# Turning more GRU state by DMA in a four-layer graph network, with a new planned order

## The chip, the cores and the metric

The kernel runs on one core of a Trainium2 chip. A core has a matrix engine (TensorE, PE in the profile; PEld is its loading of weights), a vector engine (VectorE, DVE), a scalar engine (ScalarE, ACT), GpSimd (POOL) and SyncE (SP), which here only issues DMAs. Each engine works through its own list of instructions in order and waits on semaphores for the others. The metric is device time in microseconds of one execution; the time of a kernel is the median of its runs.

## The reference

The input is 64 graphs of 256 nodes with 256 features in float32, and for each graph a 256 x 256 adjacency matrix of zeros and ones. Four layers follow each other, each of the form `x = x + f(relu(layernorm(x)), adj)`:

- layer 0: graph attention with 4 heads of 64. Scores are leaky-ReLU of a source score plus a destination score, masked by the adjacency, softmax over neighbours, then ELU.
- layer 1: graph attention with 4 heads, ReLU and a second layer norm over each head.
- layer 2: graph attention with one head of 256.
- layer 3: a gated graph network with three rounds, which share the GRU weights:

```
for i in range(3):
    m = h @ weight[i]
    aggr = A.T @ m
    h = gru_cell(aggr, h)     # r, z = sigmoid(...), n = tanh(i_n + r * h_n), h = (1 - z) * n + z * h
```

All is float32 in the reference.

## The kernel before

The 64 graphs are taken in 33 units: the first and the last hold one graph, the 31 between hold two (`units`, line 853). For a unit the function `graphs` (line 1053) records the operations of `layer0`, `layer1`, `layer2` and `gru`. Nothing runs while it records: `op` (line 600) notes an engine, a cost in ns, the buffers read and written, and a function that will emit the instructions. Most operations are emitted through a helper, so the profile shows them at line 906.

The planner `_Schedule` then sets the order. `plan` (line 696) walks backwards from the end that each unit is given, `(first + nb) * PACE / 2` (line 1664), and gives each operation a due time. `run` (line 706) simulates the engines with the recorded costs: whenever an engine is free it starts the operation with the earliest due time whose inputs are done and whose buffers are free. The order found is the order in which the instructions are written out, for every engine and for the queues on which SP and ACT issue DMAs. Constants shape it: `HOP` is the time from the end of an operation until others may use it, `RESERVE` multiplies costs, `DMA_LATENCY` (3500 ns) and `DMA_RATE` price a DMA, `YIELD` says when DVE leaves the SBUF port that it shares with GpSimd. Buffers come from classes with fixed counts (line 888): for example 5 `xt` (the rows of a unit), 8 PSUM banks, 2 `hl`, one `am_r`, 2 `y`, 3 `pl`, 2 `tp`. Classes in `STRICT` (only `hl`) are not given to a later unit while an earlier one still has to take one.

Attention. Rows are normalised (`norm`), turned so that features lie on partitions (`transposed`), and multiplied by the weights (`project`, line 1200). Attention weights are products of exponentials, so each needs one multiplication and a maximum (`weights`, line 1291). A head can be "lifted": ACT computes the first part (line 1306) and DVE one fused operation per 256 columns. Otherwise DVE does a multiplication with maximum (line 1297) and a minimum with the mask. `LIFTED0` names the lifted heads for units 0 to 2, `LIFTED` for the others.

The GRU. State and aggregate are held with features on partitions, in two halves j = 0, 1 of 128 features. `gate` (line 1551) multiplies gate weights with the state `ht` (weights `whh`) or the aggregate `ag` (weights `wc`): two products, each seen in the trace as two MATMUL records. In a round, `unit` (line 1615) computes each half of the new state `h_new`. For the next round its rows are needed with nodes on partitions: `rows_of` (line 1581) turns a half and `split` (line 1511) writes it as a high part and a remainder (`hl`), rounded to a format that PE multiplies faster; `aggregate` (line 1525) multiplies by the adjacency (`am_r`) and copies the result to `ag`.

A half is turned in one of two ways. On PE: four transposes into a PSUM bank (line 1590). By DMA, in `rows_turned` (line 1560): ACT copies the float32 half into two planes of 16-bit numbers (`pl`, line 1149), SP issues a DMA that transposes 2-byte elements (`tp`, line 1570), and DVE joins the planes into `y`. For units 1 to 31 (`BACK`) the DMA way is used for both halves after the last round and for the halves named in `EARLY` after rounds one and two. The first and last unit use PE. After the last round the turned half is added to `xt`, and the unit's `xt` is stored by one DMA (line 1653). `transposed` uses the same three steps for units 3 to 31.

At the start the gate biases `bih` and `bhh` are loaded on ACT's queue (lines 961 and 962) and added on DVE by `gate_biases` (line 1044).

Of the kernel before, what the change touches and what calls it, by code (L numbers as in the profile page):

```python
# [14 lines left out]
OP = mybir.AluOpType  # L15
# [507 lines left out]
CLOSED = 0  # L523
CENTRED = ()
BACK = range(1, 32)
EARLY = (0,)
HEADS = 3
LIFTED0 = (0,)
CENTRED0 = ()
SPLIT_DVE = ()  # L530
JOIN_DVE = ("y",)
HI_DVE = False
MERGED = True
LIFTED = (0,2)
LEAVE = 0
PACE = 97000.0


def _runs(numbers):
# [15 lines left out]
class _Op:  # L555
    __slots__ = (
        "engine", "cost", "port", "emit", "group", "bufs", "takes", "nbytes", "succs", "waits", "due", "ready",
        "index", "yields", "base", "grabs", "leave", "halves",
    )


class _Schedule:
# [9 lines left out]


    OVERLAP = {"pe": 0, "act": 97, "dve": 81, "pool": 0, "sp": 0}
    HOP = {"pe": 300, "act": 100, "dve": 60, "pool": 100, "sp": 0}
    DMA_LATENCY = 3500
    DMA_RATE = 220.0
    DMA_AHEAD = 2000
    RESERVE = {"dve": 1.0, "act": 1.03}
    STRETCH = 1.0  # L580
    MARGIN = 1600
    YIELD = 5000.0
    GUARDED = ("wh","cb2_")
    STRICT = ("hl",)
    STICK = 0.0
# [12 lines left out]
        return _Buf(cls, shape, dtype, tile)  # L598

    def op(self, engine, cost, emit, reads=(), writes=(), takes=(), nbytes=0, port=False, yields=False,  # L600
           grabs=False, leave=0, halves=False):
        o = _Op()
        o.leave, o.halves = leave, halves
        o.port, o.yields, o.grabs = port or grabs, yields, grabs
        o.engine, o.base, o.emit, o.group, o.nbytes = engine, cost, emit, self.group, nbytes
        o.cost = cost * self.RESERVE.get(engine, 1.0)
        o.succs, o.index, o.ready = [], len(self.ops), 0.0
        deps, o.bufs, o.takes = set(), [], []
        for written, items in ((False, reads), (True, writes)):
            for item in items:  # L610
                b, part = item if isinstance(item, tuple) else (item, None)
                if b not in o.bufs:
                    o.bufs.append(b)
                    b.left += 1
                if written and b.tile is None and b not in o.takes:
                    o.takes.append(b)
                keys = list(b.parts) if part is None else [k for k in (part, None) if k in b.parts]
                for k in keys:
                    writer, readers = b.parts[k]
                    if writer is not None:  # L620
                        deps.add(writer)
                    if written:
                        deps.update(readers)
                writer, readers = b.parts.get(part, (None, []))
                if written:
                    if part is None:
                        b.parts.clear()
# [68 lines left out]
    def plan(self):  # L696
        for o in reversed(self.ops):
# [2 lines left out]
                if s.group == o.group or o.group not in self.end or o.group < 0:  # L700
                    late = min(late, s.due - self.STRETCH * s.cost - self.MARGIN)
            if o.nbytes:
                late -= self.DMA_LATENCY + o.nbytes / self.DMA_RATE
            o.due = late

    def run(self):
# [28 lines left out]
        while True:  # L735
# [74 lines left out]
def _fast_path(  # L810
# [86 lines left out]
    buf, op = sched.buf, sched.op  # L897
# [17 lines left out]
    def dma(engine, nbytes, emit, reads=(), writes=(), takes=(), cost=None):  # L915
        op(engine, cost or (450 if engine == "sp" else 320), emit, reads, writes, takes, nbytes)

    a_t = [buf("ag", [P, 2, H, E]) for _ in range(2)]
    a2_t = buf("o", [P, 4, H, E])
# [133 lines left out]
    def graphs(u, first, nb):  # L1053
# [165 lines left out]
        def factors(wh, heads, width, slope, shift):  # L1219
# [29 lines left out]
                for h in range(heads):  # L1249
                    spread(h)  # L1250
            else:
                ps, row, rd = bank(), buf("row", [R, P]), buf("rd", [R, P])

                def emit_t():
                    nc.tensor.transpose(  # L1255
                        ps.tile[:R, :P], wh.tile.rearrange("p h c w -> p (h c) w")[:, :, width + 1], ident
                    )

                op("pe", 109, emit_t, [wh], [ps])

                def emit_row():
                    nc.scalar.activation(
                        row.tile, ps.tile[:R, :P], AF.Exp, scale=slope - 1.0, bias=-shift * (slope - 1.0)
                    )

                op("act", 260, emit_row, [ps], [row])
                dma("act", 1 << 13, lambda: nc.scalar.dma_start(rd.tile, row.tile), [row], [rd])

                def broadcast(k, cb):
                    dma("sp", K * nb << 17, lambda: nc.sync.dma_start(  # L1270
# [234 lines left out]
        def gru(pair):  # L1505

            xt, hns, am_h = pair["xt"], pair["hn"], pair["am"]
            am = buf("am_r", [P, C, N], F32R)
            vec(nc.vector.tensor_copy, dve(683), lambda: am.tile, lambda: am_h.tile, reads=[am_h], writes=[am], port=True)

# [70 lines left out]
            def rows_of(ht, j, last):  # L1581
# [27 lines left out]
            for i in range(L):  # L1609
# [51 lines left out]

    for u, (first, nb) in enumerate(units):
        sched.group = u
        sched.end[u] = (first + nb) * PACE / 2
        graphs(u, first, nb)


# [70 lines left out]
```

## Time and profile before

| | us |
|---|---|
| median of 3 runs | 3004.19 (3002.52 to 3005.85) |
| the profiled execution's own time | 3004.92 |
| its span, first to last instruction | 3003.1 |
| mean granted TensorE clock | 0.998 |
| gates, line 1553: busy | 2124.5 in 4752 MATMUL records |
| transposes of state, line 1590: busy | 41.8 in 272 |
| ACT copies into pl from the state | 128.9 in 124 (1040 ns each) |
| DVE copies into y | 91.1 in 124 (735 ns each) |
| DMA transposes tp<-pl of all layers | 356 issues |

A line of the profile's groups gives source line, engine, operation, output and inputs by the program's names, and shapes. Matmuls are pipelined and their ends are modelled, so the busy time of a short group includes a drain that overlaps the next one; in the chain of work each group is counted only until the next begins. SPq marks an instruction that SP's queue issues. A wait is put down to the semaphore that came last.

### The profile page before, as it was taken

To read this page: it belongs to the slowest core of one execution; us is meant where nothing else is said; L and a number is where in the kernel's file an instruction comes from. 1 tells how busy PE (TensorE), PEld (TensorE's weight loads), DVE (VectorE), ACT (ScalarE), POOL (GpSimd) and SP (SyncE) were. 2 spreads that over 40 slices of the span, in tenths; PEclk is the share of its full clock that TensorE was granted. 3 is DMA by queue.
4 is the path that set the end of the run, shared out by engine and by line. 5 is a ranking of instruction groups with operands and counts; after the bars stand their busy time and mean duration, and the time that the engine had idled before them with its cause. 6 is when DMAs were issued, how large, how long until landed. Compare 5 with 4: busy or idle time off the path is not lost.

```text
span 3003.1 us, 47684 instructions
## 1 busy us (share of the span) xinstructions
PE 2969.4 (99%) x17175; PEld 1783.2 (59%) x17175; DVE 2330.5 (78%) x5547; ACT 2313.0 (77%) x4321; POOL 279.5 (9%) x317
## 2 busy tenths in 40 slices
PE   8999999999999999999999999999999999999998
PEld 6765556555556556566555565556565565565555
DVE  7878877778877788877778777788777788777754
ACT  7867788778788787878878788787887877776653
POOL 2101001011010101000100100110101010000000
PEclk9999999999999999999999999999999999999999
DMA  4323333434343333334333244343333333322210
GB/s 131 79 57 73 76 85 78 92 67 97 71 92 71 85 86 76 89 79 81 92 69 91 67 85 92 74 93 72 91 68 85 88 79 78 77 57 68 46 38 19
DMA packets 494793, 232.12 MB, mean 77 GB/s; under 512 B 421642, under 2 KB 474452, under 8 KB 494548
## 3 DMA queue, kind: packets, MB, share of 16 engines
q1 hardware_dynamic: 490576, 227.62, 33.2%
q8 instruction: 138, 2.26, 0.3%
q10 hardware_dynamic: 3972, 1.36, 0.2%
q14 instruction: 107, 0.88, 0.1%
HBM read 109.84 MB, written 17.34 MB: 42 GB/s over the span
## 4 chain that ended last, share of the span: by engine, by line
PE 98%; DVE 1%; ACT 0%; DMA 0%; issue 0%; SPq 0%; ACTq 0%; DVEq 0%
PE bank L1553 66%; PE bank L1332 12%; PE bank L1200 12%; PE bank L1532 6%; PE bank L1590 1%; PE bank L1026 1%; PE bank L1235 0%; PE bank L1161 0%; PE bank L1255 0%; DMA w0e<-in_L_gnn_W_dram 0%; DVE o L906 0%; DVE g L906 0%; ACT g L906 0%; DVE xt L906 0%; DVE ht L906 0%
## 5 line engine op out<-in xcount | busy, mean ns | idle before, releaser
L1553 PE MATMUL bank<-ht,whh 128*128 128x512 f32 (+1 forms) x2376 | 1064.5, 580 | 0.8 <-ACT ht L906 0.8
L1553 PE MATMUL bank<-ag,wc 128*128 128x512 f32 (+1 forms) x2376 | 1060.0, 581 | 0.0
L1553 PEld LDWEIGHTS bank<-ag,wc 128*128 128x128 f32 x2376 | 446.4, 190 | 499.2 <-issue 479.5
L1553 PEld LDWEIGHTS bank<-ht,whh 128*128 128x128 f32 x2376 | 436.7, 190 | 442.2 <-issue 424.6
L906 ACT ACTIVATE g<-bank,bg 128x512 f32<-128x512 f32 (+1 forms) x594 | 396.5, 672 | 241.7 <-PE bank L1553 236.3
L906 DVE SCALAR_TENSOR_TENSOR g<-g,g 128x512 f32<-128x512 f32 (+1 forms) x396 | 264.8, 669 | 353.5 <-ACT g L906 351.2
L1332 PEld LDWEIGHTS bank<-wh,pt 128*64 128x64 f32 (+1 forms) x8704 | 342.6, 141 | 82.6 <-issue 64.7
L1332 PE MATMUL bank<-wh,pt 128*64 128x65 f32 (+1 forms) x8704 | 373.1, 232 | 1.7 <-DVE pt L906 1.7
L1306 ACT ACTIVATE pt<-cb,f 128x256 f32<-128x256 f32 x620 | 328.8, 588 | 1.9 <-DMA cb<-rd 1.8
L906 DVE SCALAR_TENSOR_TENSOR pt<-pt,f,cap 128x256 f32<-128x256 f32 x620 | 272.3, 478 | 68.0 <-ACT pt L1306 67.8
L1149 ACT COPY ht<-tp 128x1024 uint16<-128x1024 uint16 x232 | 304.6, 1339 | 1.3 <-DMA tp<-pl 1.3
L1210 ACT ACTIVATE wh<-bank,mv 128x264 f32<-128x264 f32 (+1 forms) x384 | 176.5, 479 | 122.7 <-PE bank L1200 121.9
L1532 PE MATMUL bank<-am_r,hl 128*128 128x256 f32 x1536 | 251.5, 312 | 0.0
L906 POOL TENSOR_TENSOR mv<-mv,nhalf 128x4 f32<-128x4 f32 (+1 forms) x132 | 146.6, 1111 | 1093.1 <-DVE mv L1091 733.2
L1149 ACT COPY pl<-xn 128x1024 uint16<-128x1024 uint16 x232 | 234.9, 1039 | 0.0
L1532 PEld LDWEIGHTS bank<-am_r,hl 128*128 128x128 f32 x1536 | 201.5, 189 | 52.9 <-issue 41.7
L906 ACT ACTIVATE g<-g,bg 128x512 f32<-128x512 f32 (+1 forms) x198 | 139.7, 707 | 95.1 <-DVE g L906 90.8
L906 DVE BATCH_NORM_STATS2 st<-xt 128x6 f32<-128x256 f32 x512 | 183.1, 411 | 7.0 <-DMA xt<-in_x_dram 6.0
L1297 DVE TENSOR_SCALAR pt<-cb,f 128x256 f32<-128x256 f32 x532 | 184.3, 407 | 4.1 <-ACT cb L1243 3.6
L906 POOL TENSOR_TENSOR mean<-mean,nhalf 128x8 f32<-128x8 f32 (+1 forms) x66 | 114.6, 1743 | 739.4 <-DVE mean L906 714.3
L1105 ACT ACTIVATE xn<-xt,mv 128x256 f32<-128x256 f32 x384 | 167.5, 496 | 4.9 <-DVE mv L906 4.1
L906 ACT COPY ag<-bank 128x512 f32<-128x512 f32 (+1 forms) x198 | 109.0, 566 | 79.9 <-PE bank L1532 79.6
(100 smaller groups left out, 3217.8 us busy)
## 6 DMA issues: line engine op xcount, KB each, us to landing
cb<-rd SPq DMA_DIRECT2D x120, 512.0 KB
xt<-in_x_dram SPq DMA_DIRECT2D x31, 512.0 KB
at<-in_adj_dram SPq DMA_DIRECT2D x31, 512.0 KB
out_dram<-xt SPq DMA_DIRECT2D x31, 512.0 KB
cb<-rd SPq DMA_DIRECT2D x34, 256.0 KB
tp<-pl SPq DMA_TRANSPOSE x356
cap<-cap_n SPq DMA_TRANSPOSE x128
rd<-row ACTq DMA_DIRECT2D x60, 8.0 KB
```

The lines of the kernel that those rows point to most:

```text
L906: emit = lambda: fn(*[a() if callable(a) else a for a in args], **kw)
L1026: nc.tensor.matmul(ps.tile[:, :D], lhsT=w3[i].tile[:, ec, dc * P : (dc + 1) * P], rhs=wih[k].tile[:, ec, :], start=(ec == 0), stop=(ec == ...
L1105: op("act", 505, lambda: nc.scalar.activation(view(), xt.tile[:, c, :], AF.Relu, bias=mv.tile[:, 3, c : c + 1], scale=2.0 if MERGED else 1 ...
L1149: op("act", cost, lambda: nc.scalar.copy(to(), of()), reads, writes)
L1200: nc.tensor.matmul(ps.tile[:, : heads * W], lhsT=ht.tile[:, c, dc, :], rhs=we[:, dc].rearrange("p h w -> p (h w)"), start=(dc == 0), stop= ...
L1210: op("act", 470, lambda: nc.scalar.activation(wh.tile[:, :, c, :], ps.tile[:, : heads * W].rearrange("p (h w) -> p h w", h=heads), AF.Iden ...
L1297: nc.vector.tensor_scalar(pt.tile[:, b, jc, :].rearrange("p (i n) -> p i n", n=P), cb.tile[:, k, 2 * b : 2 * b + 2, :], f.tile[:, 1, h, c ...
L1306: op("act", 590, lambda: nc.scalar.activation(view().rearrange("p (i n) -> p i n", n=P), cb.tile[:, k, 2 * b : 2 * b + 2, :], AF.Relu, sca ...
L1332: nc.tensor.matmul(ps[q * Q : (q + 1) * Q], lhsT=pt.tile[:, b, jc, i0 : i0 + Q], rhs=wh.tile[:, h, 2 * b + jc, :w], start=(jc == 0), stop= ...
L1532: nc.tensor.matmul(ps.tile[:, b * N : (b + 1) * N], lhsT=rows(k, b, sc), rhs=am.tile[:, 2 * b + sc, :], start=(k == 0 and sc == 0), stop=( ...
L1553: nc.tensor.matmul(by_chunk(ps.tile[:, :S]), lhsT=w[:, dc, g * P : (g + 1) * P], rhs=block(v, dc), start=(first and dc == 0), stop=(last a ...
L1590: nc.tensor.transpose(ps.tile[:, c * P : (c + 1) * P], ht.tile[:, j, c * P : (c + 1) * P], ident)
```

## The change

- `EARLY` becomes (0,1): after rounds one and two the second half too is turned by DMA in units 1 to 31.
- `LIFTED0` becomes (0,2): head 2 of layers 0 and 1 is lifted for units 0 to 2.
- A DMA can carry a `lag`, a further time by which the planner takes it to land later. The two bias loads get 6000 ns.
- The last unit stores each half of its features when that half is done, instead of one store at the end.
- Buffers: xt 5 to 6, xn 4 to 3, y 2 to 1, pl 3 to 2, tp 2 to 3; a class `col` is declared.
- Planner: PACE 97000 to 100000, HOP of PE 300 to 250 and of DVE 60 to 100, RESERVE of ACT 1.03 to 1.0, YIELD 5000 to 0, a DVE plane copy costed at 738 for 690.
- A second way to form `rd` (`by_columns`) is written but `SCATTER` is False, and `FIRST` is 0, so neither has an effect.

```
-EARLY = (0,)
+EARLY = (0,1)
 HEADS = 3
-LIFTED0 = (0,)
+LIFTED0 = (0,2)
...
+SCATTER = False
 LIFTED = (0,2)
 LEAVE = 0
-PACE = 97000.0
+PACE = 100000.0
+FIRST = 0.0
+LAG = 6000
...
-    HOP = {"pe": 300, "act": 100, "dve": 60, "pool": 100, "sp": 0}
+    HOP = {"pe": 250, "act": 100, "dve": 100, "pool": 100, "sp": 0}
...
-    RESERVE = {"dve": 1.0, "act": 1.03}
+    RESERVE = {"dve": 1.0, "act": 1.0}
...
-    YIELD = 5000.0
+    YIELD = 0.0
...
             if o.nbytes:
-                late -= self.DMA_LATENCY + o.nbytes / self.DMA_RATE
+                late -= self.DMA_LATENCY + o.lag + o.nbytes / self.DMA_RATE
...
-                        post(self.dma_free + self.DMA_LATENCY, "done", o)
+                        post(self.dma_free + self.DMA_LATENCY + o.lag, "done", o)
...
-            "xt": (slots, 5), "at": (slots, 1), "am": (slots, 6), "cap": (slots, 4),
-            "cap_n": (slots, 1), "xn": (slots, 4), "ht": (slots, 2), "wh": (slots, 3),
+            "xt": (slots, 6), "at": (slots, 1), "am": (slots, 6), "cap": (slots, 4),
+            "cap_n": (slots, 1), "xn": (slots, 3), "ht": (slots, 2), "wh": (slots, 3),
...
-            "hl": (slots, 2), "am_r": (slots, 1), "g": (slots, 8), "y": (slots, 2), "f": (slots, 6),
-            "st": (slots, 4), "mv": (slots, 6), "row": (slots, 3), "rs": (slots, 10),
-            "mean": (slots, 4), "pl": (slots, 3), "tp": (slots, 2), "rd": (dram, 4), "bank": (banks, 8),
+            "hl": (slots, 2), "am_r": (slots, 1), "g": (slots, 8), "y": (slots, 1), "f": (slots, 6),
+            "st": (slots, 4), "mv": (slots, 6), "row": (slots, 3), "col": (slots, 4), "rs": (slots, 10),
+            "mean": (slots, 4), "pl": (slots, 2), "tp": (slots, 3), "rd": (dram, 4), "bank": (banks, 8),
...
-    dma("act", 1 << 12, lambda: nc.scalar.dma_start(bi.tile, bih), (), [bi])
-    dma("act", 1 << 12, lambda: nc.scalar.dma_start(bh.tile, bhh), (), [bh])
+    dma("act", 1 << 12, lambda: nc.scalar.dma_start(bi.tile, bih), (), [bi], lag=LAG)
+    dma("act", 1 << 12, lambda: nc.scalar.dma_start(bh.tile, bhh), (), [bh], lag=LAG)
...
-                vec(nc.vector.tensor_copy, 690, to, of, reads=reads, writes=writes, port=True)
+                vec(nc.vector.tensor_copy, 738, to, of, reads=reads, writes=writes, port=True)
...
+            halved = u == len(units) - 1
...
                 vec(nc.vector.scalar_tensor_tensor, dve(685), lambda: xt.tile[:, :, block], view, 0.5,
-                    lambda: xt.tile[:, :, block], op0=OP.mult, op1=OP.add, reads=[ps], writes=[xt])
+                    lambda: xt.tile[:, :, block], op0=OP.mult, op1=OP.add,
+                    reads=[ps, *(parts(xt, range(C)) if halved else [])], writes=[(xt, ("j", j)) if halved else xt])
+                if halved:
+                    dma("sp", nb << 17, lambda: nc.sync.dma_start(
+                        out_v[:, chunks, block], xt.tile[:, :, block]), [(xt, ("j", j))], [])
...
-            dma("sp", nb << 18, lambda: nc.sync.dma_start(out_v[:, chunks, :], xt.tile), [xt], [])
+            if not halved:
+                dma("sp", nb << 18, lambda: nc.sync.dma_start(out_v[:, chunks, :], xt.tile), [xt], [])
```

More of the change, by code (lines that the diff above doesn't have):

```diff
@@ L557 @@
         "engine", "cost", "port", "emit", "group", "bufs", "takes", "nbytes", "succs", "waits", "due", "ready",
-        "index", "yields", "base", "grabs", "leave", "halves",
+        "index", "yields", "base", "grabs", "leave", "halves", "lag",
     )
@@ L600, in op @@
     def op(self, engine, cost, emit, reads=(), writes=(), takes=(), nbytes=0, port=False, yields=False,
-           grabs=False, leave=0, halves=False):
+           grabs=False, leave=0, halves=False, lag=0):
         o = _Op()
-        o.leave, o.halves = leave, halves
+        o.leave, o.halves, o.lag = leave, halves, lag
         o.port, o.yields, o.grabs = port or grabs, yields, grabs
@@ L913, in _fast_path, with dma @@
     B_ids = const(ident)
-    def dma(engine, nbytes, emit, reads=(), writes=(), takes=(), cost=None):
-        op(engine, cost or (450 if engine == "sp" else 320), emit, reads, writes, takes, nbytes)
+    def dma(engine, nbytes, emit, reads=(), writes=(), takes=(), cost=None, lag=0):
+        op(engine, cost or (450 if engine == "sp" else 320), emit, reads, writes, takes, nbytes, lag=lag)
     a_t = [buf("ag", [P, 2, H, E]) for _ in range(2)]
@@ L1251, in factors, with by_rows, emit_t, emit_row @@
             else:
[L1252 to L1267, printed above, removed]
+                rd = buf("rd", [R, P])
+                def by_rows():
+                    ps, row = bank(), buf("row", [R, P])
+                    def emit_t():
+                        nc.tensor.transpose(
+                            ps.tile[:R, :P], wh.tile.rearrange("p h c w -> p (h c) w")[:, :, width + 1], ident
+                        )
+                    op("pe", 109, emit_t, [wh], [ps])
+                    def emit_row():
+                        nc.scalar.activation(
+                            row.tile, ps.tile[:R, :P], AF.Exp, scale=slope - 1.0, bias=-shift * (slope - 1.0)
+                        )
+                    op("act", 260, emit_row, [ps], [row])
+                    dma("act", 1 << 13, lambda: nc.scalar.dma_start(rd.tile, row.tile), [row], [rd])
+                def by_columns():
+                    col = buf("col", [P, heads, C])
+                    op("act", 225, lambda: nc.scalar.activation(
+                        col.tile, wh.tile[:, :, :, width + 1], AF.Exp,
+                        scale=slope - 1.0, bias=-shift * (slope - 1.0),
+                    ), [wh], [col])
+                    dma("act", 1 << 13, lambda: nc.scalar.dma_start(
+                        rd.tile.rearrange("r p -> p r"), col.tile.rearrange("p h c -> p (h c)"),
+                        allow_slow_non_contiguous=True), [col], [rd], lag=9000)
+                by_columns() if SCATTER else by_rows()
                 def broadcast(k, cb):
@@ L1663, in _fast_path @@
         sched.group = u
-        sched.end[u] = (first + nb) * PACE / 2
+        sched.end[u] = (first + nb) * PACE / 2 - (FIRST if u == 0 else 0.0)
         graphs(u, first, nb)
```

## The prediction

> **What bounds the kernel now.** I read the page's busy times and its chain first.
>
> ```profile
> span 3003.1 us, 47684 instructions
> PE 2969.4 (99%) x17175; PEld 1783.2 (59%) x17175; DVE 2330.5 (78%) x5547; ACT 2313.0 (77%) x4321; POOL 279.5 (9%) x317
> ```
>
> PE was busy for 2969.4 of 3003.1 us, and the chain of work that ended last is PE for 98% of the span. Only 33.7 us are not PE's. The next view, busy time by stretch, says where those lie (columns: stretch, its length, then busy us and instruction count of PE, PEld, DVE, ACT and POOL, granted clock, DMA share, GB/s).
>
> ```profile
> 0.00:100.00 100.00, 78.79 (x767) 64.97 (x768) 82.37 (x260) 75.22 (x201) 22.66 (x39) 0.97 0.41 114
> 100.00:2900.00 2800.00, 2799.65 (x16059) 1659.60 (x16059) 2205.54 (x5193) 2196.82 (x4042) 254.78 (x275) 1.00 0.35 78
> 2900.00:3004.00 104.00, 90.93 (x351) 58.67 (x349) 42.63 (x96) 40.98 (x78) 2.03 (x3) 0.98 0.08 19
> ```
>
> The head loses 21.2 us of PE, the tail 12 to 13, and the 2800 us between 0.35. In that middle ACT and DVE have a fifth of their time free, and the granted clock is 1.00. So what leaves PE in the middle leaves the span, as long as the next instruction of PE's fixed list is ready. Whether it is turns on the layer boundary of the GRU; the timeline shows one (start us, us, engine).
>
> ```profile
> 634.12 1.23 SPq L1570 DMA_TRANSPOSE tp<-pl  x1
> 641.14 0.68 DVE L906 SCALAR_TENSOR_TENSOR ht<-g,g 128x512 f32<-128x512 f32 x1
> 641.90 0.71 DVE L906 COPY y<-tp 128x1024 uint16<-128x1024 uint16 x1
> 643.28 0.60 PE L1590 MATMUL bank<-ident,ht 128*128 128x128 f32 x4
> 644.40 0.56 ACT L1519 CAST hl<-bank 128x512 fp32r<-128x512 f32 x1
> 647.74 0.67 DVE L906 TENSOR_TENSOR hl<-bank,hl 128x512 fp32r<-128x512 f32 x1
> 649.45 1.51 PE L1532 MATMUL bank<-am_r,hl 128*128 128x256 f32 x8
> 651.50 0.56 ACT L906 COPY ag<-bank 128x512 f32<-128x512 f32 x1
> 654.26 1.88 PE L1553 MATMUL bank<-ag,wc 128*128 128x512 f32 x4
> ```
>
> The second half of the state is ready at 641.82, is turned on PE at 643.28, and the first gate that needs its aggregate runs at 654.26: 12.4 us, in which PE did other work. The first half went by DMA; its copy into y ran 6.5 us after its issue ended.
>
> **The change, part by part.**
>
> *The PE transposes removed.* Units 1 to 31 turn the second half after layers one and two: 62 groups of four transposes, 248 of the 272 at line 1590. In the chain a group takes 0.44 us, so 62 x 0.44 = 27.3 us. From the other side: by line 1590's busy time, 41.8 us for 272, a group is 0.61, or 38 us; but that counts the drain, which overlaps the next matmul. Without unit 31's two groups, which lie in the tail, it is 26.4. I take -27.3.
>
> *The work added in their place.* Each group now needs a pl copy on ACT (1.04 us), a transpose on SP's queue (1.24 to issue, and by the trace's semaphore records a median of 1.83 more to land), a y copy on DVE (0.735), and the split from y instead of from PSUM (ACT 0.613 for 0.583; DVE 0.680 for 0.676). Over 62 groups ACT gains 64.5 + 1.9 = 66 us, DVE 46, SP's queue 77. In the middle (60 groups) ACT goes from 2197 to 2261 us and DVE from 2206 to 2250, in a stretch shortened to 2774: 82% and 81%. They lie beside PE; I cost them at nothing while PE stays the fullest. If that cover went, the price would be the latency below.
>
> *The latency added at a boundary.* Before: 0.60 + 0.58 + 0.68 = 1.9 us from state to split rows. After: 1.04 + 1.24 + 1.83 + 0.74 + 0.61 + 0.68 = 6.1. That is 4.3 us more, 266 us if all 62 were bare. Cover: in the boundary shown, 641.82 + 6.1 + 0.95 for the aggregate + 0.59 for its copy + about 0.7 for hand-overs gives 650.2, still 4 us before the consumer. At the next boundary the state is ready at 677.92, so the aggregate would be copied by 686.3, where it now is copied by 688.75. Further cover: six hidden-state gates of 1.72 us each depend only on the state; three had run by 654.26. What is late next is the aggregate's copy, not PE. I take 0. Bounds: nothing, to 1 us bare at every boundary (+62).
>
> *What queues behind the new waits.* On ACT the 124 pl copies that wait for the state cost 11.6 us of idling over 29 waits; 62 more make about 6 us, free at 82%. On DVE no y copy waited visibly. On SP a transpose stands in the queue until ACT has filled pl, and loads behind it stand too; yet ACT's lifted weights waited only 1.9 us in all for broadcast loads. I take 0; bounds 0 and +6 from that ACT row.
>
> *Head: second lifted head, later biases.* For units 0 to 2 head 2 of layers 0 and 1 moves from four 0.407 copies and a 1.215 minimum to four 0.588 activations on ACT and four 0.478 on DVE. Counting unit 0 as half size, DVE loses 4.8 us and ACT gains 11.8. From 81.7 to 95.5 us the chain runs mostly over DVE with PE waiting, so relief there can reach PE. Bounds -4.8 (all of it) and +11.8 (all of ACT's). I take -1: the nearest row is that DVE stretch, but only part of the relief precedes it. The bias additions ran at 11.60 directly behind another DVE operation: 0, within 1 us either way.
>
> *The tail.* Unit 31's two groups get the longer path where little else runs. State ready at 2905.64: the aggregate comes at about 2914.0, its consumer now starts at 2912.34, and hidden-state gates are left to fill. Ready at 2932.95: 2941.3 against 2940.61. I take +1; bounds 0 and +6. The last store was issued at 2997.45 and SP saw it land by 3001.50; half of it leaves earlier now, but its data comes from a first half finished 0.7 us before. I take -0.3; bounds -1.5 (the fastest store of the run landed 2.17 us after its issue, this one 3.66) and +0.5 (one more 0.39 us issue).
>
> *Buffers and planner constants.* xt 5 to 6, xn 4 to 3, y 2 to 1, pl 3 to 2, tp 2 to 3, and new costs, hand-over times and pace. No instruction changes; the order does, and no row prices one order against another. Bounds: -12 (over half of the head's idle) to the +62 above; I take 0, since the middle idles 0.35 us in 2800 and a boundary has 4 us of room.
>
> *Sum.* The profiled execution took 3004.9 us (span 3003.1): 3004.9 - 27.3 - 1 + 1 - 0.3 = 2977.3. It stood 0.7 above the median, 3004.19, so about 2977.
>
> *A rule that speaks against it.* The row: a group holds PE 0.44 us, and the DMA takes 1.24 + 1.83 us, held by no compute engine. The Trainium skill's "VectorE: DVE Perf Modes", "The three transpose paths" and "Rules for kernel authors", puts a 128x128 bf16 transpose at 390 ns on TensorE and 1309 ns by DMA, and says to use TensorE when a PSUM destination is acceptable. It is acceptable here. An estimate by that page: eight two-byte blocks by DMA are 10.5 us against 1.6, so 62 x 8.9 = +552 us. The rule compares latencies and doesn't ask which engine is full, so I go by the row.
>
> **The rivals.**
>
> *Slower: the boundary becomes bare.* PE runs its list in order. The GRU uses most of PE (line 1553 alone is 66% of the chain), and with one am_r and the strict hl rule a unit's GRU hardly overlaps the next one's. If the planner finds too little other work within 6 us, or one y or three xn hold it back, each of 62 boundaries stalls. At 1 us that is +62: 2977 + 62 = 3039. It decides from 0.44 us a boundary, where the gain is gone. For it: 4.3 us are added where the room was 4. Against: the trace's 6.5 us from issue to y in the boundary shown did no harm.
>
> *Part of the gain is lost.* ACT is fullest at 75.6 of 91 us (691 to 782) and would reach 78 of 90. If its in-order list makes PE wait 0.25 us at each boundary, 62 x 0.25 = 15: 2992.
>
> *No change.* The relief is taken by another limit, say the wait for the unit's own aggregate, at 0.44 us a boundary: 3004. For it: the removal shortens PE, not the GRU's chain. Against: the room of 4 us.
>
> *More gain.* The new order also closes head idling, up to 12 us: 2965.
>
> **How the numbers follow.** Forecast 2977, its own range 2966 to 2986 (head -10, tail and queues +9): 0.60. More gain, below 2964: 0.02. Part lost, 2986 to 2998: 0.10. No change: 0.07. Slower: 0.21, with about 0.17 beyond 3012. A measurement of this kernel tells about 0.2%, 6 us, from no change. Faster is 0.60 + 0.02 + 0.10 = 0.72. The range runs from 2964 to 3012, leaving out 0.02 and 0.17.
>
> **What would show it.** Line 1590 with 24 transposes, 186 y copies, PE busy near 2942 us; the middle still without PE waits, ACT and DVE near 82%. PE waits at lines 1532 or 1553 on hl or ag, repeating every 30 to 45 us, would show the slower rival. The prediction is wrong if the middle idles over half a microsecond at a boundary.

## The result and the profile after

The changed kernel took 2992.4 us (median of 6 runs, 2989.96 to 2994.56), the kernel before beside it 3004.73 (3002.52 to 3006.56). The ratio is 0.9959, 95% interval 0.9947 to 0.9972: 12.3 us faster. I had forecast 2977, so 27 us faster. The direction and the range (2964 to 3012) held, the size did not: less than half of the gain arrived.

The profiled execution of the changed kernel took 2989.96 us, the fastest of its six and 2.4 under their median; that of the kernel before took 3004.92. Between these two the difference is 15.0 us. From the page, the busy times and the line of the copies that feed the new transposes:

```profile
span 2988.0 us, 47508 instructions
PE 2952.2 (99%) x16927; PEld 1751.9 (59%) x16927; DVE 2380.5 (80%) x5603; ACT 2367.7 (79%) x4403; POOL 274.9 (9%) x317
...
L1152 ACT COPY pl<-ht 128x1024 uint16<-128x1024 uint16 x186 | 193.5, 1042 | 6.1 <-DVE ht L909 5.9
```

The instructions are as announced: 186 copies for 124 on ACT, and 248 PE instructions fewer (17175 to 16927). Of the line that turned state on PE, now line 1608, 24 instructions are left (shortest, median and longest in ns, then the first and last start in us):

```profile
L1608 PE MATMUL bank<-ident,ht x24: 272/273/327, 113.1 to 2981.4; 128*128 128x128 f32 x24
```

ACT and DVE took the work without becoming full (79% and 80%). But PE's busy time fell by 17.2 us, from 2969.4 to 2952.2, where I had said "near 2942". The busy time by stretch (columns: stretch, length, then busy us and count of PE, PEld, DVE, ACT and POOL, granted clock, DMA share, GB/s) shows that this isn't a matter of waiting:

```profile
0.00:100.00 100.00, 79.36 (x781) 66.47 (x782) 81.12 (x260) 81.43 (x213) 23.73 (x39) 0.98 0.42 112
100.00:2900.00 2800.00, 2796.14 (x15846) 1634.01 (x15845) 2261.33 (x5264) 2249.86 (x4120) 250.32 (x276) 1.00 0.37 84
2900.00:2988.00 88.00, 76.68 (x305) 51.45 (x303) 38.05 (x81) 36.46 (x70) 0.80 (x2) 0.97 0.10 24
```

PE idles 20.6 us in the head (21.2 before), 3.9 in the middle (0.35), 11.3 in the tail (12.2 of the 103.1 us to the span's end). That is 2 us more idling in all. The clock is the same. So PE was busy, with fewer instructions, for some 10 us longer than my sum has it. What was it busy with?

**Where the time is.** The timeline of PE shows it (start us, us, line, instruction, count). The attention of layers 0 and 1 multiplies with 64 columns of weights, half of the array's width: `128*64`, 64 records for an operation on two heads. In the kernel before, two such operations often stand back to back:

```profile
726.69 1.88 PE L1553 MATMUL bank<-ag,wc 128*128 128x512 f32 x4
728.50 3.96 PE L1332 MATMUL bank<-wh,pt 128*64 128x65 f32 x128
732.39 2.01 PE L1200 MATMUL bank<-w2e,ht 128*128 128x258 f32 x8
```

In the changed kernel they mostly stand alone, with gates between:

```profile
726.32 3.60 PE L1571 MATMUL bank<-ht,whh 128*128 128x512 f32 x8
729.84 2.09 PE L1349 MATMUL bank<-wh,pt 128*64 128x65 f32 x64
731.86 1.98 PE L1571 MATMUL bank<-ht,whh 128*128 128x512 f32 x4
733.78 2.08 PE L1349 MATMUL bank<-wh,pt 128*64 128x65 f32 x64
735.79 3.70 PE L1571 MATMUL bank<-ht,whh 128*128 128x512 f32 x8
```

Read the starts. A gate record starts every 0.429 us in a long row of them, so four take 1.72 us; the four between the two half-width stretches take 731.86 to 733.78, 1.92. The last record before a stretch and the first behind it each hold PE some 0.1 us longer. And 128 half-width records in one stretch take 3.89 us, two stretches of 64 take 2 x 2.02 = 4.04 (the second: 733.78 to 735.79, 2.01). Over the trace, from the start of the last gate record ahead of a stretch to the start of the second behind it, the median is 3.072 us with 64 half-width records (17 times) and 4.942 with 128 (23 times). So 64 records cost 4.942 - 3.072 = 1.870, and entering and leaving costs 3.072 - 1.870 - 2 x 0.429 = 0.344 us a stretch. Stretches of 32 records check that this doesn't hang on the length: the sum gives 0.935 + 0.858 + 0.344 = 2.137, and the two such in the changed kernel with gates around them take 2.140 and 2.141.

Counted in the trace as unbroken rows of `128*64` records, there are 77 stretches before and 113 after. 36 x 0.344 = 12.4 us. With the 27.3 us of transposes that makes -14.9 us of PE work, and the two profiled executions differ by 15.0. That was an account of two traces; the runs below test it.

### The profile page after: what moved, and what is told of

Read it like the earlier page. It is cut to its first block, busy times and chain, and to the rows that moved or that the text cites. A ratio compares the mean times of both kernels' runs of the same rounds, so it can differ in the third digit from the quotient of the medians.

```text
span 2988.0 us, 47508 instructions
## 1 busy us (share of the span) xinstructions
PE 2952.2 (99%) x16927; PEld 1751.9 (59%) x16927; DVE 2380.5 (80%) x5603; ACT 2367.7 (79%) x4403; POOL 274.9 (9%) x317
## 4 chain that ended last, share of the span: by engine, by line
PE 97%; ACT 2%; DVE 1%; issue 0%; DMA 0%; POOL 0%; DVEq 0%; ACTq 0%; POOLq 0%
PE bank L1571 66%; PE bank L1349 12%; PE bank L1203 11%; PE bank L1550 6%; PE bank L1029 0%; ACT ht L1152 0%; ACT g L909 0%; PE bank L1260 0%; PE bank L1164 0%; ACT pt L1323 0%; PE bank L1238 0%; DVE g L909 0%; DVE pt L909 0%; DMA xt<-in_x_dram 0%; DVE ht L909 0%
## 5 line engine op out<-in xcount | busy, mean ns | idle before, releaser
L1571 PE MATMUL bank<-ht,whh 128*128 128x512 f32 (+1 forms) x2376 | 1051.0, 581 | 3.2 <-ACT g L909 1.2
L1571 PE MATMUL bank<-ag,wc 128*128 128x512 f32 (+1 forms) x2376 | 1042.3, 581 | 0.0
L1349 PE MATMUL bank<-wh,pt 128*64 128x65 f32 (+1 forms) x8704 | 380.6, 232 | 0.0
L1550 PEld LDWEIGHTS bank<-am_r,hl 128*128 128x128 f32 x1536 | 200.7, 188 | 50.2 <-issue 33.7
L1108 ACT ACTIVATE xn<-xt,mv 128x256 f32<-128x256 f32 x384 | 174.7, 504 | 30.9 <-DVE mv L909 29.4
L1152 ACT COPY pl<-ht 128x1024 uint16<-128x1024 uint16 x186 | 193.5, 1042 | 6.1 <-DVE ht L909 5.9
L909 DVE SCALAR_TENSOR_TENSOR g<-bank,g 128x512 f32<-128x512 f32 (+1 forms) x198 | 132.9, 671 | 80.6 <-PE bank L1571 80.6
L909 DVE BATCH_NORM_STATS2 st<-xt 128x6 f32<-128x256 f32 x512 | 189.1, 415 | 5.9 <-DMA xt<-in_x_dram 5.7
L1213 ACT ACTIVATE wh<-bank,mv 128x264 f32<-128x264 f32 (+1 forms) x384 | 169.1, 483 | 20.7 <-PE bank L1203 19.0
```

The lines of the kernel that those rows point to most:

```text
L909: emit = lambda: fn(*[a() if callable(a) else a for a in args], **kw)
L1108: op("act", 505, lambda: nc.scalar.activation(view(), xt.tile[:, c, :], AF.Relu, bias=mv.tile[:, 3, c : c + 1], scale=2.0 if MERGED else 1 ...
L1213: op("act", 470, lambda: nc.scalar.activation(wh.tile[:, :, c, :], ps.tile[:, : heads * W].rearrange("p (h w) -> p h w", h=heads), AF.Iden ...
L1349: nc.tensor.matmul(ps[q * Q : (q + 1) * Q], lhsT=pt.tile[:, b, jc, i0 : i0 + Q], rhs=wh.tile[:, h, 2 * b + jc, :w], start=(jc == 0), stop= ...
L1550: nc.tensor.matmul(ps.tile[:, b * N : (b + 1) * N], lhsT=rows(k, b, sc), rhs=am.tile[:, 2 * b + sc, :], start=(k == 0 and sc == 0), stop=( ...
L1571: nc.tensor.matmul(by_chunk(ps.tile[:, :S]), lhsT=w[:, dc, g * P : (g + 1) * P], rhs=block(v, dc), start=(first and dc == 0), stop=(last a ...
```

## The experiments

Differences are medians against runs of the kernel before on the same chip, which took 3004.6 to 3004.9 us. Theory A is that the new order has more half-width stretches, each at 0.344 us; theory O, formed after the first four runs below, that the planner's order as a whole sets the waits, so that any edit brings others. The rivals stand in each expectation.

**The turning alone.** The kernel before with `EARLY` alone.

```
-EARLY = (0,)
+EARLY = (0,1)
```

> The kernel before with EARLY = (0,1) and nothing else of the change. Its order has 127 stretches of half-width attention matmuls on PE, against 77 in the kernel before and 113 in the changed one. Theory A (each such stretch costs PE 0.344 us of entering and leaving, as the trace of before shows: gate to gate 3.072 us with 64 records between, 4.942 with 128): -27.3 for the transposes, +50 x 0.344 = +17.2, so about -10 us against the kernel before, 2995. Theory B (the stretches cost nothing extra; each of the 62 longer boundaries takes back 0.2 us in short waits): -27.3 + 12 = -15, 2990. Theory C (EARLY gives all of its gain; buffers and planner constants took part of it back): -27, 2977.

Measured: 3069.29 us (3067.11 to 3070.75), ratio 1.0212, interval 1.0198 to 1.0225. No theory had that: 64.5 us slower. PE's waits (line waited at, releaser: us in all, times, longest):

```profile
PE bank L1553 <- ACT ag L906: 27.5, 14, 2.2
PE bank L1332 <- issue: 22.5, 12, 1.9
```

and the middle of it, in the view by stretch:

```profile
100.00:2900.00 2800.00, 2745.87 (x15560) 1611.52 (x15559) 2204.46 (x5158) 2202.98 (x4033) 241.36 (x271) 0.99 0.37 83
```

PE idles 54.1 us there. With 127 stretches theory A gives -27.3 + 50 x 0.344 = -10.1, so 74.6 us are left over. Of these 54.7 are idling of PE (span less busy time, 88.4 for 33.7); the rest is counted as busy, since a matmul's modelled end covers a short wait: the interval with 64 half-width records that has a median of 3.072 us, as elsewhere, has a mean of 3.61 here. The largest wait is a gate's wait for the copied aggregate, the very wait that my slower rival named; the second line is idling for which the profile shows no releaser. So that rival is real in this order, for 27.5 of the 74.6 us, and under these planner constants `EARLY` gains nothing without the change's other edits.

**All but the turning.** The changed kernel with the second halves turned on PE again.

```
-EARLY = (0,1)
+EARLY = (0,)
```

> The changed kernel with EARLY = (0,) again: the same transposes on PE as the kernel before, all else as changed; 111 half-width stretches. Theory A: +34 x 0.344 = +11.7 us, about 3016. Theory B: no longer boundary and no transpose saved, so as the kernel before, 3005. Theory C: the constants cost 12 us, 3017, and so it agrees with A here.

Measured: 3112.97 us (3111.11 to 3115.39), ratio 1.0358, interval 1.0344 to 1.0373; 108.2 us slower. Again no theory had it. It has 111 stretches, so A's part is 34 x 0.344 = 11.7 us; 96.5 us are left over, 69 of them idling of PE (102.8 for 33.7), this time at other places:

```profile
PE bank L1349 <- DVE pt L909: 19.1, 4, 11.9
...
PE bank L1608 <- DVE ht L909: 11.4, 12, 2.9
PE bank L1203 <- ACT ht L1152: 11.3, 6, 3.5
PE bank L1550 <- ACT g L909: 9.4, 3, 3.1
```

One half of the change costs 65 us, the other 108, and together they gain 12. Effects that add up can't do that. Each kernel gets a fresh order from the planner, and what is measured is that order.

**An order with fewer stretches.** The planner already knows half-width operations (`halves`); it prefers to stay with one kind among operations whose due times lie within `STICK` of each other, and can price a switch with `SWITCH`. Both are 0 in both kernels. Here the first is set in the changed kernel.

```
-    STICK = 0.0
+    STICK = 8000.0
```

> The changed kernel with STICK = 8000: on PE the planner prefers an operation of the same width if its due time is within 8 us of the most urgent one. 82 half-width stretches instead of 113, all instructions as in the changed kernel. Theory A: 31 x 0.344 = 10.7 us less than the changed kernel, 2982, unless the order makes PE wait. Theory B: as the changed kernel, 2992. Theory C: as the changed kernel, 2992.

Measured: 2991.78 us (2990.92 to 2994.5), ratio 0.9958, interval 0.9944 to 0.9972: as the changed kernel, -13.0 against the kernel before. It has 82 stretches, so A gives -27.3 + 1.7 = -25.6 of PE work, and 12.6 us are left over; 7.5 of them are idling of PE (41.2 for 33.7). PE's busy time did fall below the changed kernel's, but by 3.9 us (2948.3 for 2952.2) where 31 stretches fewer make 10.7, and the middle idles 8.9 us for 3.9:

```profile
PE bank L1203 <- ACT ht L1152: 7.1, 11, 3.5
```

The stretches fell and the time stayed. That fits an order that is a bargain between stretches and waits, but by itself it can't tell A from a stretch that costs nothing.

**The price of a stretch by itself.** Two kernels settle that. Both are the kernel before with one needless 128x128 transpose more in each of 132 attention operations; its result is overwritten. In the first it stands ahead of the operation, where it parts two that stood back to back; in the second between the two heads of an operation, where it cuts every one. The order of all else is that of the kernel before.

```
             def emit():
+                nc.tensor.transpose(banks_[0].tile[:, :P], ident, ident)
                 for ps, pt, h in zip(banks_, pts, hs):
```

> The kernel before with one more full-width transpose of the identity on PE at the start of each of the 132 attention operations, into a bank that is then overwritten; the order is else that of before. 132 stretches instead of 77. Theory A: 132 x 0.109 = 14.4 for the transposes and 55 x 0.344 = 18.9 for the stretches, +33 us, 3038. If a stretch costs nothing extra: +14, 3019.

```
                 for ps, pt, h in zip(banks_, pts, hs):
+                    if h == hs[1]:
+                        nc.tensor.transpose(ps.tile[:, :P], ident, ident)
                     for c in range(C):
```

> The kernel before with the same 132 dummy transposes as in dummy_between_ops, but each put between the two heads of an attention operation, where it cuts a run of half-width matmuls in two; what it writes is overwritten by the next matmul. Added PE work is the same in both (132 x 0.109 = 14.4 us), the number of half-width runs is 209 there against 132. Theory A (each half-width run costs 0.344 us to enter and leave): 14.4 + 132 x 0.344 = 59.8 us over the kernel before, about 3064, and 77 x 0.344 = 26.5 us over dummy_between_ops. Rival (a foreign matmul costs its own time and something fixed wherever it stands, whatever stands around it): as dummy_between_ops, about 3036. Rival (the run's cost is an artefact of this trace's records): 3019.

Measured: the first 3035.94 us (3035.65 to 3036.55), ratio 1.0103 (1.0087 to 1.0118), 31.2 us slower where A said 33; the second 3057.4 (3056.2 to 3058.43), ratio 1.0175 (1.0159 to 1.019), 52.6 slower where A said 59.8. The same 132 instructions cost 21.5 us more in the one place than in the other, by 77 stretches: 0.279 us each. Less the transposes' own 14.4 us (132 x 0.109, from the 0.44 of a group of four), the first has 16.8 us for 55 stretches, 0.305 each, the second 38.2 for 132, 0.290. That the cost is nothing is out. It is 0.28 to 0.31 us where the neighbour is a short transpose and 0.344 by the starts where it is a 512-wide gate. In the timeline of the second:

```profile
701.27 1.15 PE L1332 MATMUL bank<-wh,pt 128*64 128x65 f32 x32
702.36 0.33 PE L1345 MATMUL bank<-ident 128*128 128x128 f32 x1
702.62 2.09 PE L1332 MATMUL bank<-wh,pt 128*64 128x65 f32 x64
704.63 0.33 PE L1345 MATMUL bank<-ident 128*128 128x128 f32 x1
```

The transpose holds PE from 702.36 to 702.62, 0.26 us, where one of a group of four takes 0.11.

This agrees with a sentence of the Trainium skill, "TensorEngine Tiling (Array Packing)", "Key Properties": that a change of the tiling mode, not of the tile alone, makes the engine drain, if going to 64 columns is such a change, which the trace doesn't name. It gives no duration; here it is about 0.3 us for going in and out.

**Does the order hang on everything?** The changed kernel with the lifted heads of units 0 to 2 as before, an edit that touches the first 100 us alone.

```
-LIFTED0 = (0,2)
+LIFTED0 = (0,)
```

> The changed kernel with the lifted heads of units 0 to 2 as before (head 0 only). It touches only the first 100 us directly. Theory O (the order as a whole is what sets the waits, and any edit at all gives another order from there to the end): the planner's own list for it leaves PE 182 us of gaps in the middle against 9 in the changed kernel's, of which about 0.85 came true elsewhere, and 98 half-width runs instead of 113 (-5 us): 2992 - 5 + 150 = about 3140. Rival (the lifted heads matter where they stand, in the head): within 5 us of the changed kernel, 2987 to 2997.

Measured: 3142.68 us (3140.17 to 3144.31), ratio 1.0456, interval 1.044 to 1.0472. An edit in the first 3% costs 150 us over the changed kernel, and PE waits in the middle:

```profile
PE bank L1550 <- ACT hl L1537: 27.2, 9, 9.9
PE bank L1550 <- DVE o L909: 21.6, 5, 9.8
```

The first line is the aggregate's wait for the split rows, the other wait that my slower rival named (line 1532 before). So the planner's order isn't local: an early difference changes it to the end, and in each 500 us from 500 to 2500 PE idles 17 to 29 us. It also means that what the lifted heads are worth where they stand can't be read from this run. The table puts the runs together. "Gaps planned" is PE's idle time from 100 to 2850 us in the planner's own simulated list, summed from the list that the kernel's program makes; "left over" is the measured difference less the two terms of PE work.

| kernel | stretches | transposes and switches | measured | left over | gaps planned |
|---|---|---|---|---|---|
| before | 77 | 0 | 0 | 0 | 2.1 |
| changed | 113 | -27.3 + 12.4 | -12.3 | 2.6 | 9.4 |
| STICK 8000 | 82 | -27.3 + 1.7 | -13.0 | 12.6 | 30.2 |
| EARLY alone | 127 | -27.3 + 17.2 | +64.5 | 74.6 | 106.5 |
| all but EARLY | 111 | 0 + 11.7 | +108.2 | 96.5 | 116.2 |
| LIFTED0 as before | 98 | -27.3 + 7.2 | +137.9 | 158.0 | 182 |

The left-over column follows the last, and the places agree too. Take the time from one PE operation's start to the next one's, and set it against the median for operations of the same planned cost. All that lies over 0.5 us above it in the middle of `EARLY` alone (77.9 us) and of all but `EARLY` (83.4 us), and 130.5 of 131.1 us in the last kernel, lies within three PE operations of a planned gap of 0.3 us or more; only 16 to 21% of the operations lie so near one. So the waits that cost 75 to 158 us stand in the plan already. They are the planner's choice of order under those constants and buffers, and not a delay on the chip that it didn't know of.

**Is there room at the boundary?** The changed kernel's order kept on every engine, with the new transposes issued twice, and four times, to the same place.

```
+                def turn():
+                    for _ in range(2 if j and not last else 1):
+                        nc.sync.dma_start(
...
-                dma("sp", 1 << 18, lambda: nc.sync.dma_start(
...
+                dma("sp", 1 << 18, turn, [pl], [tp], cost=1250)
```

> The changed kernel with each of the 62 new DMA transposes issued twice on SP's queue, the same data to the same place, in an otherwise unchanged order on every engine. The split rows of the second half then come at least 1.23 us later (one more issue; 3.1 if the second waits for the first to land). Theory R (a boundary has some 4 us of room in the order as it is): no more than 6 us above the changed kernel, 2990 to 2998. Rival (the boundary is bare and the change's lost 15 us are latency there): 62 x 1.23 = 76 us more, about 3069.

> As tp_twice, with each new transpose issued four times: 3.7 us later at least, 9.2 if each waits for the one before to land. Theory R: 3.7 us lie just within the room of 4, so 2992 to 3020; if each waits to land, 9.2 - 4 = 5.2 us bare at most boundaries, up to 62 x 5.2 = 322 us more, and SP's queue then holds back the loads behind it as well. Rival (the boundary is bare): 62 x 3.7 = 229 us more, about 3221, and three times what tp_twice shows.

Measured, twice: 2998.62 us (2996.94 to 3002.96), ratio 0.9982, interval 0.9972 to 0.9992. That is 6.2 above the changed kernel, though each second issue waited for the first to land (the two write the same tile, and the program puts a semaphore wait between them). The waits of SP's queue at that line (67 times, 1.88 us each; the columns are as for PE's waits):

```profile
SPq L1590 <- DMA tp<-pl: 125.7, 67, 3.4
```

With its own 1.23 us a second issue delays the result by 3.1 us, 192 us over 62 boundaries, and 6 arrive at the end. First the changed kernel's boundary (SPq is SP's queue), then the same one with two issues:

```profile
641.51 1.04 ACT L1152 COPY pl<-ht 128x1024 uint16<-128x1024 uint16 x1
...
642.57 1.23 SPq L1588 DMA_TRANSPOSE tp<-pl  x1
...
649.29 0.74 DVE L909 COPY y<-tp 128x1024 uint16<-128x1024 uint16 x1
...
650.06 0.62 ACT L1537 CAST hl<-y 128x512 fp32r<-128x512 f32 x1
...
652.23 1.50 PE L1550 MATMUL bank<-am_r,hl 128*128 128x256 f32 x8
...
653.77 0.59 ACT L909 COPY ag<-bank 128x512 f32<-128x512 f32 x1 [1.84 <-PE bank L1550]
...
655.31 3.60 PE L1571 MATMUL bank<-ag,wc 128*128 128x512 f32 x8
```

```profile
642.25 1.04 ACT L1152 COPY pl<-ht 128x1024 uint16<-128x1024 uint16 x1
643.31 5.01 SPq L1590 DMA_TRANSPOSE tp<-pl  x2
...
650.03 0.74 DVE L909 COPY y<-tp 128x1024 uint16<-128x1024 uint16 x1
...
656.06 1.45 PE L1571 MATMUL bank<-ag,wc 128*128 128x512 f32 x3
```

All of the second boundary lies 0.74 us later, from the copy into pl on, and its second issue ends 3.8 us later than one alone would (5.01 for 1.23). That delay is gone by the copy into y, which in the changed kernel stands 5.5 us behind the end of the issue, while a transpose lands 1.85 us after it (median, by the trace's semaphore records). The copy had 3.6 us to spare.

Measured, four times: 3460.01 us (3458.0 to 3462.53), ratio 1.1513, interval 1.1493 to 1.1532. 468 us above the changed kernel. Theory R had up to 322 us more if each issue waits for the one before, and the bare boundary would have shown three times what two issues show, 19 us; so there was a room and it is used up. PE idles 360.7 us, 324.9 more than the changed kernel's 35.8, which is about what theory R had; beyond it PE was busy 147.8 us longer. The granted clock was 0.94, and 66 times two neighbouring gate records start 0.84 to 0.85 us apart, where 0.429 is usual; how much of the 147.8 us that makes, and how much of the idling is the boundary and how much SP's held-up loads, was not separated. The page's busy times, and the middle in the view by stretch:

```profile
span 3460.7 us, 47792 instructions
PE 3100.0 (90%) x16927; PEld 1833.1 (53%) x16927; DVE 2379.2 (69%) x5603; ACT 2371.5 (69%) x4403; POOL 274.7 (8%) x317
...
100.00:2900.00 2800.00, 2526.21 (x13783) 1481.04 (x13782) 1953.78 (x4566) 1976.81 (x3643) 220.68 (x242) 0.94 0.41 89
```

**A better order.** If stretches and waits are what the order costs, an order with few of both should give the predicted gain. Two sets of constants for the changed kernel, picked among many by planned gaps and counted stretches; the first sets a price for the switch:

```
-PACE = 100000.0
+PACE = 98000.0
...
-    HOP = {"pe": 250, "act": 100, "dve": 100, "pool": 100, "sp": 0}
-    DMA_LATENCY = 3500
+    HOP = {"pe": 200, "act": 100, "dve": 100, "pool": 100, "sp": 0}
+    DMA_LATENCY = 3000
...
-    STICK = 0.0
-    SWITCH = {True: 0.0, False: 0.0}
+    STICK = 6000.0
+    SWITCH = {True: 150.0, False: 200.0}
```

> The changed kernel with other constants in the planner alone: a price for leaving half-width matmuls, a pace of 98000, hand-over 200 for PE, DMA latency 3000. 75 half-width runs instead of 113. Theory A and O together: -38 x 0.344 = -13.1 us of PE work at about as many waits (the list leaves gaps like the changed kernel's): 2979. Rival (the waits outside the list's knowledge eat it, as in stick): 2990. Rival (half-width runs cost nothing): 2992.

The second:

```
-PACE = 100000.0
+PACE = 96000.0
...
-    HOP = {"pe": 250, "act": 100, "dve": 100, "pool": 100, "sp": 0}
-    DMA_LATENCY = 3500
+    HOP = {"pe": 300, "act": 60, "dve": 60, "pool": 100, "sp": 0}
+    DMA_LATENCY = 2500
...
-    STICK = 0.0
+    STICK = 2000.0
```

> The changed kernel with other constants in the planner alone: a smaller price for leaving half-width matmuls, a pace of 96000, hand-over 300 for PE and 60 for ACT and DVE, DMA latency 2500. 81 half-width runs instead of 113, 8 us of gaps in the middle of its list. Theory A and O: -32 x 0.344 = -11 us: 2981. Rival (hand-overs and latencies taken shorter than they are turn into waits): 2990 to 3000. Rival (half-width runs cost nothing): 2992.

Measured: 2977.77 us (2975.99 to 2979.09), ratio 0.9908, interval 0.9893 to 0.9923; and 2981.86 (2980.37 to 2985.7), ratio 0.9922, interval 0.9908 to 0.9935. Theory A and O had 2979 and 2981. Both beat the changed kernel (0.9947 to 0.9972). The page and the middle of the first:

```profile
span 2976.1 us, 47377 instructions
PE 2941.3 (99%) x16927; PEld 1754.4 (59%) x16927; DVE 2375.2 (80%) x5603; ACT 2357.7 (79%) x4403; POOL 274.5 (9%) x317
```

```profile
100.00:2900.00 2800.00, 2795.84 (x15894) 1641.79 (x15893) 2261.05 (x5274) 2245.33 (x4132) 249.19 (x278) 1.00 0.34 84
```

It has the same instructions on PE as the changed kernel (16927) and the same idling in the middle (4.2 us for 3.9), and PE is busy 10.9 us less. 38 stretches fewer at 0.344 are 13.1.

**The control.** A fair comparison gives the kernel before the same search.

```
-PACE = 97000.0
+PACE = 93000.0
...
-    HOP = {"pe": 300, "act": 100, "dve": 60, "pool": 100, "sp": 0}
-    DMA_LATENCY = 3500
+    HOP = {"pe": 250, "act": 100, "dve": 80, "pool": 100, "sp": 0}
+    DMA_LATENCY = 2500
...
-    RESERVE = {"dve": 1.0, "act": 1.03}
+    RESERVE = {"dve": 1.0, "act": 1.02}
...
-    YIELD = 5000.0
+    YIELD = 0.0
...
-    STICK = 0.0
-    SWITCH = {True: 0.0, False: 0.0}
+    STICK = 6000.0
+    SWITCH = {True: 150.0, False: 200.0}
```

> The kernel before, with nothing changed but constants in the planner (a price for leaving half-width matmuls, a pace of 93000, other hand-over times), chosen as best1's were and given the same number of tries. 70 half-width runs instead of 77. It is the control for best1. If best1's 27 us were the change's alone, nothing is to be had here: 7 x 0.344 = 2.4 us, 3002. If the choice of the order itself is worth some of it, it shows here: the list's own estimate is 10.6 us less than for the kernel before, 2994, and the change would be worth 2994 - 2978 = 16 us between two chosen orders.

Measured: 2997.07 us (2995.92 to 2997.8), ratio 0.9974, interval 0.9963 to 0.9984. The search is worth 7.8 us to the kernel before, between the two expectations. So of the 27.0 us of the best order 7.8 could be had without the change, and between the two searched orders the change is worth 2997.1 - 2977.8 = 19.3 us. With 70 stretches there and 75 here, A gives -27.3 + 5 x 0.344 = -25.6 of PE work; the remaining 6 us aren't explained by a run. The pages of the two show where they lie. The control's:

```profile
span 2995.1 us, 47763 instructions
PE 2963.3 (99%) x17175; PEld 1778.8 (59%) x17175; DVE 2333.6 (78%) x5547; ACT 2302.0 (77%) x4321; POOL 279.4 (9%) x317
```

PE idles 31.8 us there and 34.8 in the best order, which is 3 us. In the best order PE is busy 28.1 us less than in the kernel before, where A has 27.3 + 2 x 0.344 = 28.0; in the control it is busy 6.1 us less, where 7 stretches fewer make 2.4. So A's account of the best order comes out, and the other 3.7 us are a gain of the control's order that A doesn't have.

## Why the prediction was right or wrong

*The PE transposes removed, -27.3.* Right. Counted from each record's start to the next record's, without idling, the transposes of state hold PE for 30.1 us in the trace before and for 3.2 in the one after, 26.9 less. The best order, with about as many stretches as the kernel before, took 27.0 us less, though against the control it is 19.3. It was right to take 0.44 us of the chain for a group and not 0.61 of busy time.

*The work added beside PE, 0.* Right. ACT's busy time rose by 54.7 us and DVE's by 50.0, where I had 66 and 46 beside the changes in the head; in the middle they are at 80 and 81%, and PE idles 3.9 us there.

*The latency of a boundary, 0, with some 4 us of room.* Right for the order that the change has: 3.1 us more at every boundary cost 0.1 us each. Not right as a statement on the change: with `EARLY` alone PE waited 27.5 us for the aggregate's copy, in a kernel 64.5 us slower. I had read the room off one boundary of an order that was about to be replaced.

*What queues behind, 0 with +6 at most.* Nothing found against it. With SP's queue busier still, by the second issues, the whole effect was 6.2 us.

*Head -1, tail +1.* By the view by stretch, idling changed by -0.6 and -0.9 us: right within 2 us, the tail with the wrong sign. *The last store, -0.3:* no gain seen; from the last store's issue to the end of the span are 5.65 us before (2997.45 to 3003.1), and 5.83 after (2982.17 to 2988.0).

*Buffers and planner constants: "I take 0".* This is the step that failed. I wrote that no instruction changes, that the order does, and that no row prices one order against another. A row did: line 1332's records stood in the timeline in stretches of 128 and of 64, with the gates beside them 0.1 us longer; and the planner's code names the price, `SWITCH`, and sets it to 0. In place of 0 the order cost 36 x 0.344 = 12.4 us of switches, and 2.6 us are left over, against 3.5 us more idling in the middle (0.35 to 3.9): -27.3 + 12.4 + 2.6 = -12.3. My bounds for this step, -12 to +62, held it. For a plan with other constants they would not have: two of the changed kernel's neighbours lie 108 and 138 us above the kernel before.

*The rivals.* "Part of the gain is lost" gave 2992, the time measured, for another reason: ACT's list making PE wait 0.25 us at each boundary. The middle idles 3.9 us in all and not 15, so the time was hit by chance and the mechanism isn't there. "Slower" didn't happen in the changed kernel, and did, in part by its own wait, with `EARLY` alone. "More gain" by the head did not come.

*The rule on transposes.* I had set the Trainium skill's "VectorE: DVE Perf Modes", "Rules for kernel authors", against the trace, with an estimate of +552 us by its latencies. The run says -12.3, the best order -27.0, and the two searched orders differ by -19.3: the sign is that of the row, by which engine is full, and nothing near +552 came.

**What stays open.** Why one set of constants leads the planner to a plan with 2 us of gaps and another to one with 182 was not traced. The change's buffers and planner constants were not varied one by one, so which of them brought the 36 further stretches is not known. Why the control's order gains 3.7 us beyond its stretches is not explained, nor are the best order's 3 us more of idling.

## What to carry to other kernels

Where an order is made by a planner, an edit is never the edit alone: price the order too, by counting in the trace what depends on neighbours (switches, stretches, waits), and compare the change in orders that were sought with equal effort, or in one that is held fixed. On a full engine, look for time inside its busy share: the starts of its instructions show a cost that busy and idle time both hide. Room at a boundary belongs to the order in which it was read.

## What the runs showed of the hardware that I had not expected

PE pays about 0.3 us each time it goes from full-width matmuls to those with 64 columns of weights and back: 0.344 us by the starts of records among 512-wide gates, 0.28 to 0.31 by the two kernels with needless transposes. Stretches of 32, 64 and 128 records give the same price. It counts as busy time.

A second DMA transpose into the same tile costs more than its issue, since the program holds it by a semaphore until the first has landed: two issues took 5.01 us where one takes 1.23. And at 62 boundaries of 3.1 us delay each, 97% of the delay vanished in the slack behind it, while four issues cost 468 us.
